# Layer 2 of a sparse graph network: when the ends of finished blocks are stepped a second time per group of gathers

## The chip, the cores and the metric

The kernel runs on one core of a Trainium2 chip. The metric is device time in microseconds, the median of three runs. The engines: PE (TensorE) multiplies matrices, DVE (VectorE) and ACT (ScalarE) work elementwise, POOL (GpSimd) issues the indirect DMAs that gather rows, SP (SyncE) issues other DMAs. Each engine works through its own queue of instructions; semaphores order them between engines.

## The reference

A graph of 3327 nodes with 512 features passes through four layers over one adjacency matrix. Each layer's result is added to its input and normalized. Layer 0 and layer 3 are attention layers, layers 1 and 2 take means over neighbours. What matters here is layer 2 and the projection with which layer 3 begins:

```
# layer 2: the mean of the first 64 neighbours of a node, through W_nb; its own features through W_line
nb_mean = keep @ X / max(cnt, 1)
xj = leaky_relu(nb_mean @ W_nb.T + b_nb)
xi = leaky_relu(X @ W_line.T + b_line)
x  = layernorm(x + xi + where(cnt > 0, xj, 0))
# layer 3: h = x @ hamilton(W) for 4 heads of 128, scores f_src, f_dst,
# e = leaky_relu(f_src[i] + f_dst[j]) masked by adj, softmax, attn @ h
```

## The kernel before

The nodes are 26 blocks of 128. The graph is sparse except in its first rows and columns, so for each block b from 1 to 25 the kernel has a list of neighbours. Block 0 is computed densely as "row 0", and the column of block 0 is added to every block's sum.

Layer 2 has its neighbours' features already multiplied by `W_nb` at the end of layer 1, as three bf16 pieces of 512 in the DRAM table `t2_d`. A **group** is up to four gathers of 128 rows of `t2_d` into a ring in SBUF (`gl` with 15 slots and `gk` with 4). `mean_group` is a generator with three stages: issue the gathers on POOL (L1005); build the selection matrix on DVE (`select`, L1021, into `salla` or `sallb`; ACT copies an incomplete one into `few`, L1795); on PE, add three matmuls per gather into the block's PSUM sum `acc` (L1810), and three for the column of block 0 (L1802). Two sums are alive at a time. There are 54 groups for the 25 blocks; `weave` sets the order of the blocks, large and small ones mixed.

When a block's sum is complete, `second` adds a `layer2_end` to `ends`. This is a generator too. Its steps issue, in order: ACT scales the sum (L2002); DVE applies the leaky ReLU, adds the residual and takes mean and variance (L2004, L2005, L802, L804), ACT evaluates logarithm and exponential (L828, L829); DVE finishes the normalization (L835 to L837, L852) into `xres`; then it waits until `g3.opened`, `g3.spare` and `g3.free` let it on; PE transposes the block (L782) and ACT copies it (`xt`, L789); PE multiplies by layer 3's weights (`products`, L1042, two halves); ACT copies the results (`write`, L1053, L1054) and SP stores them as a row of layer 3's table `t3_d` (L770, from the single buffer `tg`). The rest of its steps belong to row 0 of layer 3 (`first_block`): ACT takes exponentials, copies the block and its mask (L1211, L1212, L1214) and sets `g3.free`; DVE makes weights (L1219, L1221); PE adds eight passes to the row-0 sum (L1224).

The layer-3 weights come from a further generator in `ends`, `score_parts`. It waits some steps for its DMAs, copies the weights in four steps (L1988, L1990), and in the last step multiplies out the score columns on DVE (`score_weights`, L1512 to L1515). Once it is done, the end of block 0 is added; its steps lead through `open_first` (L1173 to L1200), which sets `g3.opened`. Until then no other block's end gets past its wait.

`Stages.step` calls each live generator once, the oldest first. `both` steps `work`, which holds the groups, and then `ends`. The order in which the generators issue instructions is the order in the engines' queues; nothing sorts them later (`manual_schedule`). After the loop, `both` is repeated until nothing lives; then `finish` (L1075 to L1239) closes row 0, and layer 3 gathers from `t3_d`. `HASTE` is 2.

Of the kernel before, what the change touches and what calls it, by code (L numbers as in the profile page):

```python
# [540 lines left out]
HASTE = 2  # L541
# [90 lines left out]
def sparse_path(ctx, tc, flag_i, x, adj, l0_w, l0_a1, l0_a2, l1_w_self, l1_b_self, l1_w_nb, l1_b_nb,  # L632
# [26 lines left out]
    def pool_in(lay, name, bufs=1, **kw):  # L659
        return lay.enter_context(tc.tile_pool(name=name, bufs=bufs, reuse_waits="tile", **kw))  # L660
# [23 lines left out]
    def mixed():  # L684


        left, ahead = list(range(1, NB)), 0
        mean = sum(chunks_of[1:]) / len(left)
        while left:
            b = left.pop(0 if ahead >= 0 else -1)  # L690
            ahead += mean - chunks_of[b]
            yield b

    weave = list(mixed())
# [83 lines left out]
    def transposed(pool, ps, src, xsum=None, b=0):  # L778

        pt = ps.tile([P, DC, P], F32, name="pt", tag="tr")  # L780
        for c in range(DC):
            nc.tensor.transpose(pt[:, c, :], src[:, c * P:(c + 1) * P], ident)  # L782
        xt = pool.tile([P, DC, P], F32, name="xt")
        if xsum is None:
            nc.scalar.copy(xt, pt)  # L785
            return xt
        n = LAST if b == NB - 1 else P
        for c in range(DC):
            nc.scalar.activation(xt[:, c, :n], pt[:, c, :n], AF.Identity, accum_out=xsum[:, c, b:b + 1])  # L789
        if n < P:  # L790
            nc.scalar.copy(xt[:, :, n:], pt[:, :, n:])
        return xt
# [7 lines left out]
    def moments(fin, y):  # L800
        st = fin.tile([P, 6], F32, name="st")
        nc.vector.bn_stats(st, y)  # L802
        mv = fin.tile([P, 2], F32, name="mv")
        nc.vector.bn_aggr(mv, st)  # L804
        return mv
# [19 lines left out]
    def power(fin, mv):  # L825

        r0 = fin.tile([P, 1], F32, name="r0")
        nc.scalar.activation(r0, mv[:, 1:2], AF.Ln, bias=eps)  # L828
        nc.scalar.activation(r0, r0, AF.Exp, scale=-0.5)  # L829
        yield  # L830
        return newton(fin, mv, r0)
# [19 lines left out]
    def scaled(o, y, mv, rs):  # L851
        nc.vector.tensor_scalar(o, y, mv[:, 0:1], rs, ALU.subtract, ALU.mult)  # L852
# [650 lines left out]
    def by_heads(w, c, H):  # L1503

        return w[:, c].rearrange("p s (h m) -> p s h m", h=H // 2)[:, :, :, 1:1 + D // H]

    def score_weights(w, tmp, a, H, OUT):
        hh = H // 2
        for c in range(DC):
            for k in range(2):  # L1510
                pr = tmp.tile([P, 2, hh, OUT], F32, name="pr")
                nc.vector.tensor_mul(pr, by_heads(w, c, H), a[:, k].rearrange("p (s h) o -> p s h o", s=2))  # L1512
                score = w[:, c].rearrange("p s (h m) -> p s h m", h=hh)
                nc.vector.tensor_reduce(score[:, :, :, k * (OUT + 1)], pr, AX.X, ALU.add)
            nc.vector.tensor_scalar(score[:, :, :, OUT + 2], score[:, :, :, OUT + 1], GAT_ALPHA, None, ALU.mult)  # L1515
# [300 lines left out]
    ends = Stages()  # L1816

    def both():
        work.step()
        ends.step()  # L1820
# [137 lines left out]
    with ExitStack() as lay:  # L1958
        fin = pool_in(lay, "l2f", 2)
        sp = pool_in(lay, "l2s", 1)  # L1960
        ps = pool_in(lay, "l2p2", 2, space=PSUM)
        pacc0 = pool_in(lay, "l2p0", space=PSUM)

        wp = pool_in(lay, "l3w")
        w3 = wp.tile([P, DC, 2, (D + 3 * H3) // 2], F32, name="w3")
        g3 = Gat("g3", t3_d, H3, OUT3, w3, 1)
        firsts.append(wp.tile([P, 3, D], BF16, name="first2"))
        nc.sync.dma_start(firsts[0], t2_d[2:2 + P, :])

        def score_parts():  # L1970

            Q = OUT3 // 4
            raw3 = wp.tile([P, H3, 4, Q], F32, name="raw3", tag="pr")
            nc.sync.dma_start(raw3.rearrange("p h s q -> p h (s q)"), l3_w.rearrange("h p o -> p h o"))
            a3 = wp.tile([P, 2, H3, OUT3], F32, name="a3")
            for s in range(2):
                nc.sync.dma_start(a3[:, s], bass.AP(tensor=l3_a.tensor, offset=l3_a.offset + s * OUT3,
                                                    ap=[[0, P], [2 * OUT3, H3], [1, OUT3]]))
            yield
            yield  # L1980

            for c, parts in enumerate(((0, 1, 2, 3), (-1, 0, 3, -2), (-2, -3, 0, 1), (-3, 2, -1, 0))):
                yield
                for s, part in enumerate(parts):
                    o = by_heads(w3, c, H3)[:, :, :, s * Q:(s + 1) * Q]
                    src = raw3[:, :, abs(part), :].rearrange("p (s h) q -> p s h q", s=2)
                    if part < 0:
                        nc.scalar.mul(o, src, -1.0)  # L1988
                    else:
                        nc.vector.tensor_copy(o, src)  # L1990
            yield
            score_weights(w3, wp, a3, H3, OUT3)

        weights = score_parts()
        ends.add(weights)

        def layer2_end(b, acc):
            yield
            y = xres[0]
            if b:  # L2000
                y = fin.tile([P, D], F32, name="e")
                nc.scalar.mul(y, acc, rdeg[:, b:b + 1])  # L2002
                yield
                nc.vector.scalar_tensor_tensor(y, y, SAGE_ALPHA, y, ALU.mult, ALU.max)  # L2004
                nc.vector.tensor_add(y, y, xres[b])  # L2005
            mv = moments(fin, y)
            rs = yield from power(fin, mv)
            scaled(xres[b], y, mv, rs)
            yield
            while b and not (g3.opened and g3.spare and g3.free):  # L2010
                yield
            g3.free = False
            G = g3.spare.pop(0)
            xt = transposed(fin, ps, xres[b], g3.xsum, b)
            yield
            pw = g3.products(ps, xt)
            yield
            g3.write(b, fin, pw)
            if b == 0:
                yield from g3.open_first(fin, ps, pacc0)  # L2020
            yield from g3.first_block(b, fin, pw, G)
            g3.spare.append(G)

        g3.spare = [fin.tile([P, H3, OUT3 + 1], F32, name="g2", bufs=2) for _ in range(2)]
        for t in g3.spare:
            nc.vector.memset(t[:, :, OUT3:], 1.0)
        for item in nexts:
            work.add(mean_group(item, t2_d, None, second, firsts, sall))
            both()
            if item[0] in weave[-HASTE:]:  # L2030
                ends.step()
            if left0 and weights not in ends.live:
                ends.add(layer2_end(left0.pop(), None))
        while work.live or ends.live:
            both()
        assert not left0
        g3.finish(fin, ps)
        g3.divided(fin, g3.acc, bias1)
# [57 lines left out]
@with_exitstack  # L2096
def kernel(ctx: ExitStack, tc: tile.TileContext, *args):


    nc = tc.nc  # L2100
    pool = ctx.enter_context(tc.tile_pool(name="flagp", bufs=1))
    flag_i = pool.tile([1, 1], I32, name="flag_i")
    sparse_path(tc, flag_i, *args)
    again = nc.values_load(flag_i[0:1, 0:1], min_val=0, max_val=1 << 20)
    with tc.If(again > 0):
        general_path(tc, *args)
# [30 lines left out]
```

## Time and profile before

| | us |
|---|---|
| median of 3 runs | 1701.81 (1696.1 to 1703.36) |
| the profiled execution | 1795.35 |
| its span, first to last instruction | 1793.6 |
| layer 2's first gather after the last of layer 1 | 1146.9 |
| layer 2's last matmul of a sum | 1438.9 |
| last row-0 product (L1224) starts | 1471.6 |
| layer 3's first gather | 1483.7 |

The profiled execution takes longer than an unprofiled run, so a difference is read within profiles or within runs. Over the whole span PE is busy for 84%, DVE for 68%, ACT for 49% and POOL for 43%, with a mean granted PE clock of 0.932. These are means over stages with different limits; the stage in question lies between 1147 and 1484 us. A row of PE's timeline gives the start, the length, the line and what ended the idle time before it.

### The profile page before, as it was taken

The numbers are of one execution on the slowest core, as the hardware profiler recorded it, in microseconds if no ns is written. First come the engines' busy times: TensorE is split into PE (matmuls) and PEld (weight loads), VectorE is DVE, ScalarE is ACT, GpSimd is POOL, SyncE is SP. The second block draws the span as 40 slices with busy tenths as digits, with TensorE's granted clock in tenths as the row PEclk, the third lists the DMA queues.
The fourth block names the chain that finished last, engine by engine and source line by source line (L and its number), as shares of the span: only waits on it lengthen the run. The fifth ranks groups of instructions, "written<-read, shape, count | busy, mean of one in ns | idle before, by whom it ended". The sixth has DMA issues, their size and how long they took to land. (4 is left out here: it accounts for less than half of the span.)

```text
span 1793.6 us, 24341 instructions
## 1 busy us (share of the span) xinstructions
PE 1513.9 (84%) x7263; PEld 1007.8 (56%) x7298; DVE 1220.8 (68%) x3289; ACT 876.6 (49%) x2921; POOL 762.9 (43%) x904
## 2 busy tenths in 40 slices
PE   5979937789999999889999998856999984788784
PEld 4756526556666667345555554423666662666663
DVE  8989859996668788135665675537655533687896
ACT  5879645656566677311221221102444442476785
POOL 2000144555555510264545552366667106666540
PEclk9989968999999999989999998988999995999897
DMA  8787766766564531398889894387888207677761
GB/s 265 248 266 241 210 192 232 207 189 205 173 200 153 178 113 61 144 401 289 291 283 357 274 319 182 132 285 246 260 263 278 92 37 199 196 209 211 214 182 44
DMA packets 130402, 381.99 MB, mean 213 GB/s; under 512 B 22037, under 2 KB 36477, under 8 KB 130259
## 3 DMA queue, kind: packets, MB, share of 16 engines
q0 software_dynamic: 67696, 252.97, 44.8%
q1 hardware_dynamic: 62563, 127.35, 21.1%
q8 instruction: 60, 0.98, 0.2%
q14 instruction: 83, 0.68, 0.1%
HBM read 331.89 MB, written 48.37 MB: 212 GB/s over the span
## 5 line engine op out<-in xcount | busy, mean ns | idle before, releaser
L1005 POOL DMA_INDIRECT gl<-t_d,idx x270 | 270.5, 1002 | 272.2 <-DMA e_d<-es 81.0
L1005 POOL DMA_INDIRECT gt<-t_d,idx x201 | 200.5, 998 | 377.4 <-DVE g0fall L845 199.7
L1334 PE MATMUL acc<-gt,sel 128*128 128x264 f32 (+3 forms) x804 | 213.0, 412 | 3.1 <-issue 1.8
L797 PE MATMUL po<-wn,xt 128*128 128x512 f32 x416 | 193.6, 607 | 11.0 <-ACT xt L785 5.7
L1005 POOL DMA_INDIRECT gm<-t_d,idx x136 | 137.7, 1012 | 136.9 <-PE acc L1810 81.8
L1334 PEld LDWEIGHTS acc<-gt,sel 128*128 128x128 f32 (+3 forms) x804 | 154.4, 201 | 43.9 <-issue 17.0
L1334 PE MATMUL acc<-gl,sel 128*128 128x260 f32 (+3 forms) x544 | 147.6, 416 | 29.5 <-issue 21.9
L1334 PEld LDWEIGHTS acc<-gl,sel 128*128 128x128 f32 (+3 forms) x544 | 105.9, 204 | 52.4 <-issue 26.1
L797 PEld LDWEIGHTS po<-wn,xt 128*128 128x128 f32 x416 | 78.7, 195 | 94.6 <-issue 76.2
L1042 PE MATMUL po<-gt,xt 128*128 128x268 f32 x416 | 115.7, 423 | 14.8 <-ACT xt L789 11.2
L1315 DVE TENSOR_TENSOR gt<-gt,pg 128x1536 f32<-128x1536 f32 (+3 forms) x63 | 116.4, 1848 | 15.4 <-ACT sel L1310 14.7
L785 ACT COPY xt<-pt 128x512 f32<-128x512 f32 x81 | 46.7, 588 | 140.3 <-PE pt L782 108.4
L1810 PE MATMUL acc<-gm,selr 128*128 128x512 f32 (+4 forms) x324 | 107.2, 454 | 5.4 <-DMA gm<-t_d,idx 3.6
L909 DVE MAX8 cand<-val 128x8 f32<-128x464 uint16 (+32 forms) x184 | 107.7, 619 | 0.0
L1042 PE MATMUL po<-w,xt 128*128 128x262 f32 x416 | 99.5, 393 | 6.3 <-ACT xt L789 5.1
L1042 PEld LDWEIGHTS po<-gt,xt 128*128 128x128 f32 x416 | 78.4, 202 | 34.1 <-ACT xt L789 14.5
L1267 ACT ACTIVATE far<-place,nmids 128x128 int16<-128x128 int16 (+3 forms) x167 | 88.0, 544 | 18.2 <-DVE ds L1277 10.1
L797 PE MATMUL po<-wx,xt 128*128 128x512 f32 x208 | 93.7, 595 | 2.1 <-DVE t L1669 1.8
L797 PE MATMUL po<-wl,xt 128*128 128x512 f32 x208 | 93.5, 594 | 2.0 <-DVE tb L1877 1.3
L1042 PEld LDWEIGHTS po<-w,xt 128*128 128x128 f32 x416 | 78.8, 192 | 25.2 <-ACT xt L789 7.5
L782 PE MATMUL pt<-s_ident,xres 128*128 128x128 f32 x500 | 79.1, 287 | 13.3 <-DVE xres L852 10.0
L881 ACT ACTIVATE m<-ab 128x1664 bf16<-128x1664 int32 x50 | 80.2, 1605 | 16.9 <-DMA ab<-in_adj_dram 13.2
(372 smaller groups left out, 3238.8 us busy)
## 6 DMA issues: line engine op xcount, KB each, us to landing
ab<-in_adj_dram SPq DMA_DIRECT2D x25, 832.0 KB
ab<-in_adj_dram SPq DMA_DIRECT2D x25, 831.5 KB
t_d<-t SPq DMA_DIRECT2D x25, 512.0 KB
gm<-t_d POOLq DMA_DIRECT2D x25, 512.0 KB
t_d<-t SPq DMA_DIRECT2D x25, 384.0 KB
t_d<-tg SPq DMA_DIRECT2D x25, 264.0 KB
gd<-t_d SPq DMA_DIRECT2D x25, 264.0 KB
t_d<-tg SPq DMA_DIRECT2D x25, 260.0 KB
```

Of the source, the lines that this page charges most:

```text
L782: nc.tensor.transpose(pt[:, c, :], src[:, c * P:(c + 1) * P], ident)
L785: nc.scalar.copy(xt, pt)
L797: nc.tensor.matmul(po, xt[:, c, :], w[:, c], start=c == 0, stop=c == DC - 1)
L881: nc.scalar.activation(m, ab[s], AF.Sign, accum_out=half[:, s, b:b + 1])
L909: nc.vector.max(out=cand[:, s, :], in_=val[:, cuts[s]:cuts[s + 1]])
L1005: nc.gpsimd.indirect_dma_start(out=t[:m, c, :], out_offset=None, in_=table[:, :], in_offset=bass.IndirectOffsetOnAxis(ap=l.idx[:m, c0 + c: ...
L1042: nc.tensor.matmul(pw[s], xt[:, c, :], self.w[:, c, s, :], start=c == 0, stop=c == DC - 1)
L1267: nc.scalar.activation(o, place[:, (c0 + q0) * P:(c0 + q1) * P], AF.Abs, bias=l.nmid[:, k:k + 1], scale=2.0)
L1315: nc.vector.tensor_mul(Gc[:, :, :OUT], Gc[:, :, :OUT], w[:, :g].rearrange("p c (h o) -> p (c h) o", o=1).to_broadcast([P, g * H, OUT]))
L1334: nc.tensor.matmul(accs[b][s], S[:m, c, :], G[:m, c, s * hh * M:(s + 1) * hh * M], start=at + c == 0, stop=last)
L1810: nc.tensor.matmul(accs[b], chosen, parts[:, k * D:(k + 1) * D], start=at + c + k == 0, stop=k == top and at + c == n - 1)
```

## The change

In the loop over layer 2's groups, the second `ends.step()` was made when the group belonged to one of the last two blocks of `weave`. It is now made whenever more than two generators are alive in `ends`, the weights' generator included. Nothing else is changed, and `HASTE` is used for the number.

```diff
         for item in nexts:
             work.add(mean_group(item, t2_d, None, second, firsts, sall))
             both()
-            if item[0] in weave[-HASTE:]:
+            if len(ends.live) > HASTE:
                 ends.step()
             if left0 and weights not in ends.live:
                 ends.add(layer2_end(left0.pop(), None))
```

## The prediction

> **What bounds the kernel now.** I began with the windows around layer 2, cut at the events that the order of its instructions gives: the gathers' start, the end of the fourth block's sums, the opening of layer 3's row 0, the last sum, the last row-0 product. Columns: stretch, length, busy time and instructions of each engine, PE clock, DMA share, GB/s.
>
> ```profile
> 1203.00:1252.07 49.07, 31.30 (x131) 14.36 (x131) 37.31 (x97) 10.64 (x42) 33.62 (x33) 0.90 0.80 248
> 1252.07:1439.00 186.93, 183.00 (x922) 124.86 (x940) 111.25 (x276) 80.77 (x402) 96.33 (x93) 0.99 0.68 221
> 1439.00:1472.80 33.80, 28.68 (x149) 24.16 (x149) 13.29 (x40) 16.06 (x89) 0.00 (x0) 0.95 0.11 40
> ```
>
> From 1252 on PE works 183.0 of 186.9 us, while DVE has 60% and ACT 43%. POOL waits for PE there (the waits of layer 2 show "POOL gl L1005 <- PE acc L1810: 21.4" and "gk" 11.4 us): gathers run ahead until the 19 slots of the ring are full, so PE sets the pace, not the gathers. The change moves PE's work but adds and removes none: before row 0 closes, both programs have 570 sum matmuls (L1810, L1802), 208 L1042 instructions (26 blocks), 104 transposes (L782) and 104 row-0 matmuls (L1224). So the end of layer 2 moves only by the time that PE **stands idle or runs slowly**. Idle before: 49.07 - 31.30 = 17.8 us in the opening, 3.9 in the middle, 5.1 in the tail. Next, where it idles, from PE's timeline and its waits:
>
> ```profile
> 1207.26 0.82 PE L1810 MATMUL acc<-gl,few 32*128 32x512 bf16 x3
> 1219.43 2.72 PE L1810 MATMUL acc<-gl,salla 128*128 128x512 bf16 x6 [11.35 <-DVE rs L835]
> ...
> 1247.74 1.13 PE L1192 MATMUL pf<-wt,s_ones 128*128 128x512 f32 x2 [2.28 <-DVE wt L1190]
> ```
>
> ```profile
> PE po L1042 <- ACT xt L789: 3.0, 5, 1.1
> ```
>
> The first three rows are the opening; the last is PE's whole list of waits for other engines from 1253 to 1440: none for a DVE select. The 11.35 us lie behind one block of DVE work, L1512 to L1515 (score weights), which starts right after a select:
>
> ```profile
> 1202.66 0.39 DVE L1021 TENSOR_TENSOR salla<-lane,dst 128x256 fp8e4<-128x256 bf16 x1
> 1202.97 0.69 DVE L1512 TENSOR_TENSOR pr<-w,a 128x512 f32<-128x512 f32 x1
> ...
> 1214.77 0.17 DVE L1515 TENSOR_SCALAR w<-w 128x4 f32<-128x4 f32 x1
> ...
> 1218.15 0.39 DVE L1021 TENSOR_TENSOR salla<-lane,dst 128x256 fp8e4<-128x256 bf16 x1
> ```
>
> The tail has the last blocks one after another, with 0.52 us of idle in front of each L1042, and a slow first one (5.49 us where 3.80 is usual):
>
> ```profile
> 1438.18 0.82 PE L1810 MATMUL acc<-gl,few 32*128 32x512 bf16 x3
> 1438.92 0.66 PE L782 MATMUL pt<-s_ident,xres 128*128 128x128 f32 x4
> 1440.87 5.49 PE L1042 MATMUL po<-w,xt 128*128 128x262 f32 x16 [1.28 <-ACT xt L791]
> 1446.19 1.06 PE L1224 MATMUL acc<-g,wt 128*128 128x129 f32 x8
> 1447.08 0.60 PE L782 MATMUL pt<-s_ident,xres 128*128 128x128 f32 x4
> 1448.21 3.80 PE L1042 MATMUL po<-w,xt 128*128 128x262 f32 x16 [0.52 <-ACT xt L789]
> ...
> 1471.61 1.16 PE L1224 MATMUL acc<-g,wt 128*128 128x129 f32 x8 [1.75 <-DVE wt L1221]
> ```
>
> **Two rules of the Trainium skill.** "TensorE: Matmul & The Clock Gate", Part 1 (The HAM clock gate), says that PE falls to half rate after an idle window of some 3.4 us and needs as long to recover. The trace agrees after the 11.35 us (2.72 us for the six matmuls at 1219.43, where nine take 2.11 at 1225.47), but it also shows a slow 5.49 us after an idle 1.28 us. I go by the trace: gaps of one or two us count too. The same page, Architectural detail, says that ACT and DVE are strict FIFO. The 11.35 us row agrees: the ready select at 1218.15 stands behind the score weights. So I forecast from the order on each queue.
>
> **The change, part by part.** *Score weights and opening.* With the weights and two block ends waiting, a group now steps them twice, so the weights come earlier in program order. They don't start earlier in time. Ahead of them stands the DVE chain of the second block end (L2004 to L804, from 1200.38), which waits for the same ACT evaluation at 1199.66. They start at about 1202.7. What moves is what stood between: the two selects of the fifth block (384 and 256 columns) now come behind the weights. That takes 18 sum matmuls from in front of the stall, and PE has nothing from 1203.2. By row durations, queue by queue: weights end 1214.7; L835 to L852 to 1215.6; first select 1216.1, PE starts (idle 12.9). Then DVE runs two steps of ends before the next select: L2004 to L804 2.3 us, the ACT pair L828/L829 0.6, L835 to L852 1.3, ready for block 0 at 1222.9. Its transposes stand on PE ahead of the next sums: idle 4.6. L1042 of block 0 waits for ACT behind another L828 (1.1), ends 1230.8; L1173, L1174 and L1181 come at about 1232 to 1233.5, L1192 waits for L1190 until 1238.7 (idle 2.3), and L1200 ends at 1241.0. In the run before that is at 1252.07. But the changed order has then only 129 sum matmuls behind it, not 192; 63 at 0.216 us (6 in 1.30) are 13.6 us. 1252.07 - 13.6 = 1238.5, so the opening is **2.5 us behind**. With more gaps PE also runs slowly longer: I add 1 us (the slow 5.49 cost 1.7). Opening **+3.5**, from 0 (DVE's waits overlap better than my reckoning) to +8 (the gaps repeat the slow pace).
>
> *Middle.* The order of PE shows the transposes of a block directly ahead of its L1042 nine times before (four in the loop, five in the tail) and seven times after (six in the loop, one in the tail). Elsewhere sums lie between and hide the copy of xt. Two more in the loop at 0.5 us: **+1**. The second step puts row 0's weights (L1219, L1221: 1.9 us) and a whole end chain (L2004 to L852: 4.2 with its wait for ACT) between two selects in eight rounds, where it was four; PE waited for none of those four, so I take **+1** for the added four, 0 to +17 (below). The other queues: POOL's and SP's instructions are the same in number; POOL's order is the same, and on SP only the place of the one two-part store of `t_d` among 25 others moves. An extra step adds no wait to them, and ACT never waited for the store to leave `tg` free between 1260 and 1400, with blocks 8 to 9 us apart; after, at least 7.
>
> *Tail.* Behind the last sum stand five blocks' L1042 before, two after. The last block's chain (L2002 0.7, DVE 2.3, L828/L829 0.5, L835 to L852 1.1, hops 0.5) makes its xres 5.2 us after the last sum, while the block ahead keeps PE to +6.0. Left idle: 0.2 in front of the first L1042, 0.52 and the final 1.75 (which stays): 2.5 us. Before: 5.1 idle and 1.7 slow, 6.8. **-4.3**; -6 to +1, as the slow first L1042 may stay.
>
> *Behind it.* Closing row 0 (L1075 to L1239, 11 us) and layer 3's first gather at 1483.7 wait for the last row-0 product as now and move with it. Layer 3's order is the same.
>
> Sum: +3.5 + 2.0 - 4.3 = **+1.2 us**, on the profiled execution's 1795.35 (span 1793.6) 1796.6; on the median, 93.5 us shorter, **1703.0**. I scale nothing: these are differences of PE idle time.
>
> **Rivals.** *Slower.* Selects L1021 queue behind two rounds of ends on DVE, and PE waits. Place: rounds that hold L1219/L1221 and a whole chain, 1.9 + 4.2 + 0.5 = 6.6 us from select to select, against PE's 4.6 us per round (570 x 0.216 + 26 x (3.6 + 0.9 + 0.44) = 252 us in 54 groups). If the lead of one group doesn't cover it, 2 us in each of eight rounds is 16, with the opening's upper end 20: 1722. It decides from four uncovered rounds on. Against it: the four such rounds before cost nothing, and DVE has 40% free. For it: the opening shows what PE loses when a select is late.
>
> *Faster.* Early ends fill the opening. If the later gaps of the opening (17.8 - 11.35 = 6.4 us) are filled by L1042s of waiting blocks and the tail gives its 4.3 to 6, the gain is 10 to 12: 1691. Against it: opening needs four steps through DVE, PE and ACT in series whatever is waiting.
>
> *Nothing at all.* Were the gathers the pace (POOL issues one per 1.27 us at best, 165 of them from 1147 on), PE's idle time would not matter: 1702. The POOL waits speak against it. That the second step never fires is excluded by the order of PE: 57 sums earlier, five blocks' tail down to two.
>
> **How the numbers follow.** 0.5% is 8.5 us, about what a measurement of this kernel can tell from no change. The parts' bounds (0 to 8, 0 to +19, -6 to +1) sum to -6 at the low end, and the high ends hardly fall together. Near no change, my forecast with the rival of gather pace: 0.57. DVE rival, at or over 1710.3: 0.28. Filled opening, at or under 1693.3: 0.15. Predicted 1703; range 1690 to 1719, which takes in the faster rival's 1691 and most of the slower one's way to 1722.
>
> **What would show it.** Right: L1512 at about 1202 to 1203; PE idle some 13 us before about 1216; L1200 at about 1241; last sum at about 1459, last row-0 product within 15 us of it, at about 1474; PE's waits for L1021 in the middle a few us. Wrong: those waits over 8 us (slower rival); PE idle in the opening under 12 us (faster rival); gathers with no wait for PE.

## The result, and the profile after

| | before | after |
|---|---|---|
| median of 6 runs, us | 1701.19 (1696.1 to 1703.36) | 1711.78 (1708.33 to 1715.27) |
| ratio | | 1.0066, 95% interval 1.0048 to 1.0083 |
| profiled span, us | 1700.5 (profile of the first experiment) | 1711.3 |

The change costs 10.6 us. The forecast was +1.2 us, with a range up to 1719, which holds the time.

One thing has to be said ahead of the profiles. The profile of before that the prediction read (span 1793.6) is some 90 us longer than the timed runs. This is not the price of profiling, as was assumed ahead of the prediction: the profiled execution of the first experiment took 1702.24 us, as unprofiled runs do. Two of the chips used below take 1788 and 1790 us for this program without a profile, so the first profile most likely comes from a chip of that kind; the record doesn't name it. So the profile after is set here against a profile of before taken on a chip of its own pace (first experiment), and runs on slow chips are compared with one another only.

The windows around layer 2, cut at the same events: first gather, end of L1200, end of the last sum, start of L1075, which follows the last row-0 product. Columns: stretch, length, busy time and instructions of PE, PEld, DVE, ACT and POOL, PE clock, DMA share, GB/s. The kernel after:

```profile
1120.95:1193.72 72.77, 55.47 (x193) 23.82 (x192) 48.34 (x120) 13.02 (x44) 56.61 (x54) 0.92 0.86 289
1193.72:1409.92 216.20, 212.59 (x1086) 144.00 (x1086) 125.75 (x313) 93.10 (x465) 115.63 (x112) 0.99 0.70 227
1409.92:1431.15 21.23, 15.49 (x66) 12.51 (x65) 7.78 (x25) 7.15 (x37) 0.00 (x0) 0.79 0.07 26
```

The kernel before, unchanged, on a chip of the same pace:

```profile
1122.10:1205.01 82.91, 68.43 (x254) 29.88 (x256) 59.02 (x146) 16.99 (x55) 64.33 (x61) 0.96 0.86 286
1205.01:1388.56 183.55, 180.77 (x922) 124.73 (x939) 109.82 (x271) 80.89 (x400) 108.37 (x104) 1.00 0.74 248
1388.56:1420.58 32.02, 26.90 (x150) 22.98 (x149) 13.30 (x40) 16.06 (x89) 0.00 (x0) 1.00 0.11 43
```

The lengths can't be subtracted as they stand, since the change moves work between the stretches. 63 sum matmuls move from the opening into the middle (0.216 us each, 13.6 us), and three blocks from the tail into the middle. A block of the tail takes 5.14 us of PE: its rows follow one another every 5.66 us, of which 0.52 is idle. That is 15.4 us. With the moved work put back:

| | opening | middle | tail | sum |
|---|---|---|---|---|
| after less before, lengths | -10.1 | +32.7 | -10.8 | +11.7 |
| moved work put back | +13.6 | -13.6 - 15.4 | +15.4 | 0 |
| lost | **+3.5** | **+3.6** | **+4.6** | **+11.7** |
| forecast | +3.5 | +2 | -4.3 | +1.2 |

The first gather starts 1.15 us earlier in the profile after, by chance, so 10.6 us are left at L1075, as in the timed runs. The three terms are of one size in this pair of profiles. Other kernels with the same tail lose 3.3 and 2.5 us in it on such a chip (second and fourth experiment), so single terms are good to a us or two. The forecast's error is nearly all in the tail.

**Opening.** DVE in the kernel after, score weights and the selects around them:

```profile
1155.46 0.18 DVE L804 BATCH_NORM_AGGREGATE mv<-st 128x2 f32<-128x6 f32 x1
1155.56 0.67 DVE L1512 TENSOR_TENSOR pr<-w,a 128x512 f32<-128x512 f32 x1
...
1167.35 0.17 DVE L1515 TENSOR_SCALAR w<-w 128x4 f32<-128x4 f32 x1
...
1168.46 0.55 DVE L1021 TENSOR_TENSOR salla<-lane,dst 128x384 fp8e4<-128x384 bf16 x1
...
1173.94 0.39 DVE L1021 TENSOR_TENSOR salla<-lane,dst 128x256 fp8e4<-128x256 bf16 x1
```

The two selects of the fifth block (384 and 256 columns) now stand behind the weights, as forecast. PE over the same time:

```profile
1160.71 0.81 PE L1810 MATMUL acc<-gl,salla 128*128 128x512 bf16 x3 [0.30 <-DMA gl<-t_d,idx]
1169.07 3.99 PE L1810 MATMUL acc<-gl,salla 128*128 128x512 bf16 x9 [7.56 <-DVE salla L1021]
1175.89 0.71 PE L782 MATMUL pt<-s_ident,xres 128*128 128x128 f32 x4 [2.83 <-DVE xres L852]
...
1184.90 0.27 PE L1174 MATMUL ptm<-s_ident,mx 128*8 128x128 f32 x1 [0.96 <-DVE mx L1173]
...
1191.46 1.12 PE L1192 MATMUL pf<-wt,s_ones 128*128 128x512 f32 x2 [1.98 <-DVE wt L1190]
```

Behind the weights PE idles 7.56 us; nine sums then take 3.99 us where nine take 2.11 at full pace. In the kernel before, on a chip of this pace, the idle time there is 3.16 us, since PE has 30 sums to do while the weights run, most of them in rows of three that wait 0.3 to 0.8 us for their gather; in the kernel after it has 15:

```profile
1173.34 2.17 PE L1810 MATMUL acc<-gl,salla 128*128 128x512 bf16 x6 [3.16 <-DVE rs L837]
```

**Middle.** PE's whole list of waits for other engines between 1194 and 1410 in the kernel after:

```profile
PE po L1042 <- ACT xt L789: 2.3, 5, 0.5
PE po L1042 <- ACT xt L791: 1.3, 1, 1.3
```

No wait for a select stands in it. Idle time is 3.6 us (216.20 - 212.59), 0.8 more than before. The stretch begins with PE slow: its clock is 0.66 from 1193 to 1198, and 1.00 in the next windows of 5 us.

**Tail.** PE behind the last sum in the kernel after:

```profile
1411.31 3.70 PE L1042 MATMUL po<-w,xt 128*128 128x262 f32 x16
1417.65 1.18 PE L1224 MATMUL acc<-g,wt 128*128 128x129 f32 x8 [2.64 <-DVE wt L1221]
1418.69 1.12 PE L782 MATMUL pt<-s_ident,xres 128*128 128x128 f32 x4
1420.26 6.37 PE L1042 MATMUL po<-w,xt 128*128 128x262 f32 x16 [0.46 <-ACT xt L789]
1429.27 2.09 PE L1224 MATMUL acc<-g,wt 128*128 128x129 f32 x8 [2.64 <-DVE wt L1221]
```

And at the end of the tail in the kernel before, on a chip of the same pace:

```profile
1413.12 3.80 PE L1042 MATMUL po<-w,xt 128*128 128x262 f32 x16 [0.52 <-ACT xt L789]
1416.76 1.06 PE L1224 MATMUL acc<-g,wt 128*128 128x129 f32 x8
1419.56 1.16 PE L1224 MATMUL acc<-g,wt 128*128 128x129 f32 x8 [1.75 <-DVE wt L1221]
```

In the kernel after, two gaps of 2.64 us and one of 0.46 make 5.74 us of idle time, against 5.12 for the five blocks before. And the last L1042 takes 6.37 us where 3.80 is usual, the last row-0 product 2.09 where 1.16 is usual, the transposes 1.12 where 0.60 is: 4.0 us of slow pace. The PE clock of the tail is 0.79; before it was 1.00.

### The profile page after: what moved, and what is told of

The parts are those of the page before. It is cut to its first block, busy times and chain, and to the rows that moved or that the text cites. A ratio compares the mean times of both kernels' runs of the same rounds, so it can differ in the third digit from the quotient of the medians.

```text
span 1711.3 us, 24356 instructions
## 1 busy us (share of the span) xinstructions
PE 1505.1 (88%) x7298; PEld 1003.5 (59%) x7298; DVE 1221.4 (71%) x3289; ACT 874.7 (51%) x2921; POOL 768.9 (45%) x904
## 3 DMA queue, kind: packets, MB, share of 16 engines
q0 software_dynamic: 67696, 252.97, 46.4%
## 5 line engine op out<-in xcount | busy, mean ns | idle before, releaser
L1005 POOL DMA_INDIRECT gl<-t_d,idx x270 | 275.7, 1021 | 219.7 <-DMA e_d<-es 54.2
L1334 PEld LDWEIGHTS acc<-gt,sel 128*128 128x128 f32 (+3 forms) x804 | 155.5, 202 | 42.8 <-issue 14.5
L1334 PE MATMUL acc<-gl,sel 128*128 128x260 f32 (+3 forms) x544 | 141.9, 407 | 25.7 <-issue 13.7
L1042 PE MATMUL po<-gt,xt 128*128 128x268 f32 x416 | 112.9, 415 | 15.7 <-ACT xt L789 11.2
L1042 PE MATMUL po<-w,xt 128*128 128x262 f32 x416 | 99.5, 393 | 4.0 <-ACT xt L789 2.7
L1042 PEld LDWEIGHTS po<-gt,xt 128*128 128x128 f32 x416 | 76.3, 196 | 34.6 <-ACT xt L789 15.1
L1042 PEld LDWEIGHTS po<-w,xt 128*128 128x128 f32 x416 | 79.3, 194 | 19.6 <-ACT xt L789 4.8
```

The costliest lines, as they stand in the source:

```text
L1005: nc.gpsimd.indirect_dma_start(out=t[:m, c, :], out_offset=None, in_=table[:, :], in_offset=bass.IndirectOffsetOnAxis(ap=l.idx[:m, c0 + c: ...
L1042: nc.tensor.matmul(pw[s], xt[:, c, :], self.w[:, c, s, :], start=c == 0, stop=c == DC - 1)
L1334: nc.tensor.matmul(accs[b][s], S[:m, c, :], G[:m, c, s * hh * M:(s + 1) * hh * M], start=at + c == 0, stop=last)
```

## The experiments

Two theories stood at first. T: the thin tail costs. O: the place of the score weights in the opening costs. Every edit is shown against the kernel after, and only its lines are printed. Gains and losses by stretch are found as above, with moved work put back.

### On a chip of the pace of the timed runs

**Before, unchanged.** No edit.

> The kernel before, unchanged, for a second profile, since the first one is 94 us longer than an unprofiled run and holds a stall of ten us in which PE, ACT and POOL all stand (1183 to 1193). Both theories: span about 1700, no such stall, and from layer 2's first gather to its last row-0 product less than the first profile's 325.9 us. Theory T (the change loses in the tail): from the end of the last sum to the end of the last row-0 product 33 to 35 us with five blocks, idle and slow PE together under 7. Theory O (it loses in the opening): PE's idle time behind the score weights is well under the first profile's 11.35 us, so that the changed kernel's 7.6 + 2.8 us are the larger.

1702.24 us, span 1700.5. Its windows are shown above. Behind the weights PE idles 3.16 us where the first profile had 11.35.

**The double step only after row 0 is open.**

```diff
-            if len(ends.live) > HASTE:
+            if g3.opened and len(ends.live) > HASTE or item[0] in weave[-HASTE:] and not g3.opened:
                 ends.step()
```

> The second step is made only once g3.opened is set (len(ends.live) > HASTE), before that the old rule: the opening is instruction for instruction that of before (192 sums ahead of L1200), and behind the last sum stand two blocks, as in the changed kernel. Theory T: most of the loss stays, +6 to +11 us against before (1707 to 1712). Theory O: the loss goes, +0 to +3 us (1701 to 1704).

1703.9 us, ratio 1.0011 (1.0000 to 1.0021). Opening -1.5, middle -0.3, tail +3.3. So the doubled rounds in the middle cost nothing when the opening is that of before: 198.70 us for what before needs 183.55 + 15.4. The tail is thin here too and loses 3.3, of which the opening gives half back. The time is O's: without second steps ahead of L1200, most of the 10.6 us are gone. T's time is missed, but the tail's loss is real.

**The change, and the last five blocks held back until the last sum.**

```diff
-            while b and not (g3.opened and g3.spare and g3.free):
+            while b and (b in weave[-5:] and work.live or not (g3.opened and g3.spare and g3.free)):
                 yield
```

> The changed kernel, but the last five blocks of weave wait in front of their transposes until no group is left: the opening and most of the middle are as in the changed kernel, and five blocks stand behind the last sum as before. Theory T: the last block's chain is hidden again behind four blocks' L1042, PE keeps its pace, 4 to 8 us come back: 1704 to 1708, and idle plus slow PE behind the last sum about 7 us instead of 10 to 13. Theory O: no change against the changed kernel, 1710 to 1713.

1714.01 us, ratio 1.0080 (1.0055 to 1.0106). The tail is what it should be: PE at clock 1.00, +0.1 against before (one row-0 product, 0.9 us, has moved ahead). But the middle lost 8.3 us (9.2 less that product), 4.0 of it more idle time. Of that, 2.1 us are new waits near the end of the sums, where no L1042 is left to stand between them:

```profile
1391.33 1.47 PE L1810 MATMUL acc<-gl,sallb 128*128 128x512 bf16 x6 [0.71 <-DVE sallb L1021]
1396.12 0.82 PE L1810 MATMUL acc<-gl,sallb 128*128 128x512 bf16 x3 [1.38 <-DVE sallb L1021]
```

The time is no nearer to before's, but the run doesn't decide between the theories: its edit gives the tail back and makes the middle dearer by as much. T as the only cause falls with the run before this one, where the thin tail is there and the time is nearly before's.

**The change, and the score weights in four steps.**

```diff
-            yield
-            score_weights(w3, wp, a3, H3, OUT3)
+            for c in range(DC):
+                yield
+                score_weights(w3, wp, a3, H3, OUT3, (c,))
```

> The changed kernel with the score weights issued in four steps instead of one (four blocks of 3 us on DVE with selects between instead of one of 12); 150 sums ahead of L1200 instead of 129; two blocks in the tail. Theory O: PE's 7.6 us behind the score weights fall to under 2 and the time with them: 1704 to 1707. Theory T: the opening is worth 3 us at most and the tail stays: 1708 to 1712.

1710.55 us, ratio 1.0055 (1.0035 to 1.0076). Opening +1.5 instead of +3.5, middle +3.3, tail +2.5. PE's wait is cut in two (3.95 and 3.74 us, both for L1021), not taken away, and the time lies in T's range. O's size for this run was too large.

### On two slower chips

The next eight profiles come from two chips on which before takes 1789.7 and 1788.4 us, close enough to one another that segments are compared across them. There PE has one more long idle stretch in the opening, whatever the kernel, 10 to 16 us ahead of nine sums that then take 4.00 us; it varies from profile to profile, so the opening is cut once more, at the end of that stretch. The two profiles of before differ by 3.7 us in one stretch, so a smaller difference between two single profiles says little here.

**Before on such a chip, the change on such a chip.** No edits.

> The kernel before, unchanged, for its segments on the chip of this call: first gather to the end of L1200 (82.9 us in the earlier look at it, 105.3 in the first profile), to the last sum (+183.6 or +186.9), to the close of row 0 (+32.0 or +33.6).

> The changed kernel, unchanged, beside the others of this call. Theory (opening +3.5, middle +3.6, tail +4.6, after correction for moved work): ratio 1.005 to 1.009. Rival (the loss belongs to the condition of one chip): under 1.003 or over 1.012.

Before: one run, 1782.69 us. After: 1809.01, ratio 1.0118 (1.0086 to 1.0150), nearly twice the loss on the other chip; the interval reaches up from the theory's range into the rival's. In us, with moved work put back (63 sums for the three kernels with the weights ahead of the selects, 42 for the two without a double step beside the weights; three blocks of the tail each, but two in the last row but one; four transposes, 0.55 us, more in that row and in "until open only"):

| | gather to the stall's end | from there to L1200 | middle | tail |
|---|---|---|---|---|
| before | 46.0 | 55.2 | 187.3 | 33.6 |
| before (the first profile) | 46.4 | 58.9 | 186.9 | 33.6 |
| after | 47.4 | 61.7 | 199.4 | 34.2 |
| after, extra transposes in the tail | 44.6 | 60.9 | 199.0 | 32.7 |
| double step until open only | 46.6 | 61.7 | 188.4 | 37.1 |
| no double step beside the weights | 47.5 | 56.7 | 189.8 | 34.0 |
| the same, extra transposes | 42.5 | 58.4 | 189.6 | 32.7 |
| double step after open, not in the last four blocks | 46.1 | 57.6 | 184.6 | 32.0 |
| double step after open, extra transposes | 47.4 | 56.5 | 186.5 | 32.7 |

**No double step while the weights' generator lives.**

```diff
-            if len(ends.live) > HASTE:
+            if len(ends.live) > HASTE and weights not in ends.live:
                 ends.step()
```

> The second step is made whenever more than two generators wait, but not while the weights' generator is still alive, so that the two selects of the fifth block stand ahead of the score weights on DVE again (150 sums stand ahead of L1200 on PE, against 192 before and 129 in the changed kernel). Theory 1 (in the opening the cost is the place of the score weights ahead of those selects): no wait for L1021 of more than 1 us behind L1515, opening within 1.5 us of before's after correction for the sums; middle and tail as in the changed kernel, about +3.6 and +4.6; total 1.0040 to 1.0055, 1708 to 1712. Rival (any second step ahead of L1200 costs, whatever is behind the weights): opening +3.5 still, total 1.0065 to 1.0080, 1712 to 1716.

1795.57 us, ratio 1.0029 (1.0014 to 1.0045), under both ranges; the interval reaches into the theory's alone. The two selects stand ahead of the weights again (DVE, this kernel):

```profile
1204.85 0.53 DVE L1021 TENSOR_TENSOR salla<-lane,dst 128x384 fp8e4<-128x384 bf16 x1
1208.87 0.39 DVE L1021 TENSOR_TENSOR salla<-lane,dst 128x256 fp8e4<-128x256 bf16 x1
1209.18 0.68 DVE L1512 TENSOR_TENSOR pr<-w,a 128x512 f32<-128x512 f32 x1
```

From the stall's end to L1200 the three profiles with the weights ahead take 60.9 to 61.7 us; the two with this rule 56.7 and 58.4, the four with before's opening 55.2 to 58.9. That is 4 us between the means (61.4 against 57.5) for the place of the weights: O holds in kind. It doesn't hold as "a shorter wait behind L1515": in this kernel PE still idles 13.38 us there, as the weights run later. What it gains is the work done ahead of the weights. The rival, that any second step ahead of L1200 costs 3.5 us in the opening, is out.

**The double step only until row 0 is open.**

```diff
-            if len(ends.live) > HASTE:
+            if len(ends.live) > HASTE if not g3.opened else item[0] in weave[-HASTE:]:
                 ends.step()
```

> The second step is made on the new rule only until row 0 is open; after that the rule of before. The opening's order is that of the changed kernel, no group after it is stepped twice before the last two blocks. Theory 1 (the middle's +3.6 us is idle and slow pace that the late opening leaves behind): opening +3.5, middle still +2 to +4, tail +2 to +5 (two blocks stand behind the last sum); total 1.0050 to 1.0075, 1710 to 1716. Rival (the middle's loss is the price of the doubled rounds themselves): middle within 1 us of before, total 1.0030 to 1.0050, 1707 to 1711.

1800.06 us, ratio 1.0053 (1.0034 to 1.0072). The time lies in the theory's range, and its interval reaches into the rival's; by the stretches the rival is the better. The opening is as late as after's (61.7), but the middle takes 188.4: about 1 us over before. So a late opening alone hardly lengthens the middle. Doubled rounds that begin when row 0 is open don't either (last two rows of the table, and -0.3 on the other chip); those that begin when the weights are done cost 2 to 3 us. After has a late opening and doubled rounds, and on these chips loses 12.

**The change, and twelve more transposes in each of the tail's gaps.**

```diff
             pw = g3.products(ps, xt)
+            if b in weave[-2:]:
+                pt = ps.tile([P, DC, P], F32, name="pt", tag="tr")
+                for _ in range(3):
+                    for c in range(DC):
+                        nc.tensor.transpose(pt[:, c, :], xres[b][:, c * P:(c + 1) * P], ident)
             yield
```

> The changed kernel with twelve extra transposes of the block's own xres (L782's form, some 1.9 us, into a PSUM tile that nobody reads) behind L1042 of each of the last two blocks, where PE has 2.64 us of idle time. They add work and no dependence for anything else. Theory 1 (some 4 us of the tail are PE's slow pace after its gaps): second L1042 of the tail 3.8 to 4.5 instead of 6.37, last row-0 matmul 1.2 instead of 2.09, total 3 to 4 us under the changed kernel's, 1.0040 to 1.0050 against before, 1708 to 1711. Rival (the pace has another cause, or the extra work only displaces the gaps): 1711 to 1715, 1.0060 to 1.0085.

1802.78 us, ratio 1.0085 (1.0060 to 1.0109). The rows are what the theory asked for (PE, tail; L2021 are the extra transposes):

```profile
1472.53 1.16 PE L1224 MATMUL acc<-g,wt 128*128 128x129 f32 x8 [1.33 <-DVE wt L1221]
1473.57 0.66 PE L782 MATMUL pt<-s_ident,xres 128*128 128x128 f32 x4
1474.68 3.80 PE L1042 MATMUL po<-w,xt 128*128 128x262 f32 x16 [0.46 <-ACT xt L789]
1478.32 1.47 PE L2021 MATMUL pt<-s_ident,xres 128*128 128x128 f32 x12
1481.12 1.16 PE L1224 MATMUL acc<-g,wt 128*128 128x129 f32 x8 [1.33 <-DVE wt L1221]
```

PE works 2.9 us more, and the tail is 1.5 us shorter (32.7 against 34.2) with its clock at 1.00 (0.89 in the change on such a chip). The ratio itself lies at the upper edge of the rival's range; both ranges had been set from the other chip. Against the 1.0118 of the change on a slow chip it is lower, but the intervals overlap, so the gain of 1.5 us is shown by the rows of the tail and not by the timed runs.

**The double step after row 0 is open, but not in the last four blocks.**

```diff
-            if len(ends.live) > HASTE:
+            if g3.opened and len(ends.live) > HASTE and item[0] not in weave[-4:]:
                 ends.step()
```

> The second step is made when row 0 is open, more than two generators wait, and the group belongs to none of the last four blocks: the opening is that of before, the middle is doubled, and three blocks' L1042 stand behind or between the last nine sums. Theory 1 (opening order and a thin tail are the costs, the doubled rounds in the middle are free): opening -1.5 to 0, middle -1 to +1, tail +0 to +2, total 0.998 to 1.001, 1699 to 1704. Rival (a shorter tail costs in any form): tail over +3 as in the run with doubled rounds in the middle only, total 1.001 to 1.003.

1789.53 us, ratio 1.0005 (0.9990 to 1.0020). Three blocks stand in the tail, which takes 32.0 us, 1.6 less than before; the middle is 2.2 shorter. Within what the timed runs can tell, this is before's time. The rival (a shorter tail costs in any form) foresaw over +3 in the tail and is out by that; the interval of the ratio alone would still allow it.

**Both costs undone: no double step beside the weights, and the extra transposes.**

> Both suspected costs undone at once: no second step while the weights' generator lives, and twelve extra transposes behind L1042 of each of the last two blocks. Theory: opening 0 to -1.5, tail +1 at most instead of +4.6, middle 0 to +3; ratio 0.999 to 1.003. Rival (the double step in the middle is the cost): 1.004 or more.

The two edits are those shown above, together. 1789.17 us, ratio 1.0008 (0.9991 to 1.0025), against 1.0118 for the change on the same chip. The loss is gone to within what the runs can tell, though the middle keeps its doubled rounds (189.6, +2.3). Most of this is the rule for the weights, which alone gave 1.0029 on the other slow chip; the transposes' share can't be told from nothing by the runs, as the two intervals overlap.

**The double step after row 0 is open, and the extra transposes.**

> The second step only after row 0 is open, with the extra transposes in the tail: the opening of before, the middle of the changed rule, a tail without slow pace. Theory: opening -1.5 to 0, middle -0.5 to +0.5, tail 0 to +1; ratio 0.998 to 1.001, at most 2 us under before, too little to be told from it. Rival (the slow pace in the tail is not worth time): the 1.0011 of the run without the extra transposes.

The edits are the rule of the second experiment and the transposes. 1789.9 us, ratio 0.9998 (0.9981 to 1.0016): before's time again; the rival's 1.0011 lies in the interval too. No variant beats before by more than a measurement can tell.

What the middle of the change loses on the slow chips shows in PE's groups there. Columns: line, operation, count, busy us, mean ns, idle us ahead of it and who ended that. The change:

```profile
L1042 PE MATMUL po<-w,xt 128*128 128x262 f32 x368 | 89.3, 397 | 7.9 <-ACT xt L789 5.1 <-issue 1.5 <-ACT xt L791 1.3
L1810 PE MATMUL acc<-gl,salla 128*128 128x512 bf16 x42 | 11.7, 427 | 0.0
```

Both costs undone:

```profile
L1042 PE MATMUL po<-w,xt 128*128 128x262 f32 x368 | 86.1, 387 | 6.6 <-ACT xt L789 4.3 <-ACT xt L791 1.3 <-issue 1.0
L1810 PE MATMUL acc<-gl,salla 128*128 128x512 bf16 x27 | 6.5, 379 | 0.0
```

The same 368 L1042 take 3.2 us longer, and the first sums 427 ns instead of 379. In windows of 10 us from its start, the change has a PE clock of 0.66 in the first and of 0.83 in two later ones; the other stays at 1.00 in its first 40 us. In all the change's middle holds 9.8 us of idle time against 6.6, of which 7.9 and 6.6 stand ahead of L1042. When the 21 sums more in it (4.5 us) are taken off, its busy time is still 6.6 us longer. So two thirds of what it loses over the other kernel are slow pace, one third is idle time, in part waits for ACT's copies. Why these waits and slow pieces come only where a late opening and doubled rounds meet stays open: no run separates them.

## Why the forecast was right in range and wrong in its terms

**What bounds the kernel.** Right. PE is busy for 212.6 of the middle's 216.2 us, POOL waits for PE, and the loss is idle time and slow pace of PE. Gather pace fell as a rival: the time did move. In the opening on the faster chip PE does wait for gathers, 0.3 to 0.8 us at a time while the weights run. (The prediction's 208 L1042 and 104 row-0 matmuls are the program's; the rows of the trace have 16 and 8 to a block, twice as many, in both kernels.)

**Opening, +3.5.** Right in size (+3.5, and +3.9 in the run with five blocks held back, which has the same opening), and in kind: the weights right behind L804, both selects behind them, idle time ahead of L1192 of 1.98 us for 2.3. The sum came out: idle time is 2.8 us more than before (17.3 against 14.5) for the 2.5 forecast, and longer busy time 0.6 us (55.47 + 13.6 against 68.43) for the 1 us allowed for slow pace. The parts were off, and that they made up for one another is luck. The stall forecast as 12.9 us was worked out on a slow chip's profile, where before had 11.35; it is 7.56 in this profile, where before has 3.16. And both kernels have slow pace there: nine sums at 3.99 us for 2.11 after, twelve at 4.62 for 2.75 before.

**Middle, +2.** Measured +3.6. Uncovered L1042: 0.8 us for +1. Selects behind two rounds of ends: 0 for +1, as PE waits for none. The remaining 2.8 are not idle time; part of them, about 1.7, is the clock of 0.66 in the first 5 us. It goes with the late opening: all five profiles with the weights ahead of both selects begin the middle with 5 us at a clock of 0.50 to 0.69, and seven of the nine others at 1.00 (0.66 and 0.74 in the two left). That the late opening is its cause is not shown. The rest can't be put down to a row. Nor is it the only way to lose there: with the weights in four steps the middle begins at 1.00 and loses 3.3 us, of which 2.8 are idle time.

**Tail, -4.3.** This is the step that failed. It measured +4.6. It said that the last block's chain "makes its xres 5.2 us after the last sum, while the block ahead keeps PE to +6.0". Both halves are wrong. DVE and ACT at that time in the kernel after:

```profile
1411.63 0.71 ACT L2002 ACTIVATE e<-acc,rdeg 128x512 f32<-128x512 f32 x1
...
1414.55 0.18 DVE L804 BATCH_NORM_AGGREGATE mv<-st 128x2 f32<-128x6 f32 x1
1415.04 0.38 ACT L1053 COPY tg<-po 128x260 f32<-128x260 f32 x1 [1.32 <-PE po L1042]
...
1416.19 0.36 ACT L1214 ACTIVATE mk<-row 128x128 f32<-128x128 fp8e4 x1
1416.40 0.33 ACT L828 ACTIVATE r<-mv,s_eps 128x1 f32<-128x1 f32 x1
...
1416.90 0.69 DVE L1221 TENSOR_TENSOR wt<-wt,mk 128x512 f32<-128x512 f32 x1
1417.51 0.15 DVE L835 SCALAR_TENSOR_TENSOR rs<-mv,r 128x1 f32<-128x1 f32 x1
...
1418.09 0.55 DVE L852 TENSOR_SCALAR xres<-e,mv,rs 128x512 f32<-128x512 f32 x1
```

The chain was priced by its own instructions, as if its queues were empty. The last sum ends at 1409.99, but L2002 starts at 1411.63, behind ACT's copies of the block ahead. The variance is ready at 1414.73, but L828 starts at 1416.40, since ACT first waits for the block ahead's L1042 (1.32 us, ahead of L1053) and makes its copies. L835 starts at 1417.51, 0.55 us after L829, behind the block ahead's L1221. So xres comes 8.7 us after the last sum (1418.64), not 5.2.

The block ahead doesn't keep PE either. Its row-0 product stands on PE directly behind its own L1042 now, ahead of the last block's transposes, and its weights take 2.64 us to come (L1053 to L1221 above). An xres at +5.2 would not have filled this gap, as the product stands first in the order of PE's rows. Before, the same 2.64 us pass between the last L1042 and its product (1416.92 to 1419.56), but 0.9 of them are covered by the product of the block ahead, and for the earlier blocks all of it is covered by the next block's work. That leaves the 1.75 which the prediction took as given for the last block. So in place of 0.2 + 0.52 + 1.75 there are 2.64 + 0.46 + 2.64.

Idle 5.7 us where 2.5 was forecast: 3.2 of the 8.9 us by which the term is off. Slow pace makes up 4.0, and 1.7 more come from the base: the slow first L1042 of the prediction's profile (5.49, and 5.49 again in the later profile of before on a slow chip) is 3.80 in the profile on the faster chip, so there was nothing to gain from it. On the slow chips, where this base exists and the slow pieces came out smaller, the tail measured +0.6. The page "TensorE: Matmul & The Clock Gate" of the Trainium skill, Part 1 (The HAM clock gate), says that the window in which idleness is judged runs freely, so that the moment of a change of pace varies. The trace agrees: with this tail and its gaps of 2.64 us, the last L1042 took 3.83, 4.08, 5.00, 5.17 and 6.37 us in five profiles, and 4.08 and 6.37 are the same kernel, the change, on two chips. So the size of the 4.0 us is in part chance. The page's window of some 3.4 us is longer than this gap, and slow pace follows it all the same; the measurement decides.

**The rivals.** *Slower* came out in sign and in size: 1711.8 lies over the 1710.3 from which the prediction counted the time as this rival's, at 0.28. It did not come out by its mechanism: it put the waits for L1021 into eight rounds of the middle, at 2 us each. There were none there; such a wait came once, in the opening. That the range holds the time is therefore luck as well: its upper end was set by waits that didn't come, and the excess over the forecast came from the tail, where the prediction allowed +1 at most. *Faster* rested on the opening being filled and the tail giving 4.3 to 6; neither happened.

Of the forecast's own signs, "last row-0 product within 15 us" of the last sum failed (19.4 us), and it named the step. "PE idle in the opening under 12 us", meant as the mark of a gain, came true (7.56) with a loss: without the base of before (3.16) the length of the stall says nothing.

## What to carry to other kernels

Price a chain that is moved to the end by what stands ahead of each of its instructions on ACT and DVE, not by its own durations, and ask what PE has to do between an instruction and the one that waits for its result: five blocks in a row hid one another's waits, two did not. In the tail of this kernel a gap cost its length and then slow pace behind it, so work that is spread out can be dearer than the same work in one piece; here 1.5 us of useless transposes in each of two gaps made the stretch 1.5 us shorter. When a profile is some per cent longer than the runs, find out first whether its gaps exist in the runs: the 11.35 us that the prediction worked from were 3.16.

## What was not expected of the hardware

The same program takes 1703 us on one chip and 1788 to 1790 on two others, in 27, 35 and 36 runs. On the slow ones layer 2's opening takes 101 to 105 us in two profiles, instead of 83, among it a stretch of 10 to 16 us in which PE idles, whose cause the records don't name. The change costs a factor of 1.0066 in the runs of the result (1.0048 to 1.0083) and of 1.0118 on a slow chip (1.0086 to 1.0150). The stretches differ too: in the first it loses 3.5, 3.6 and 4.6 us in opening, middle and tail, on the slow chip some 12 in the middle and 0.6 in the tail.
